# Choosing between narrow and wide matmuls while a recurrence runs: an instruction budget in the planner, and an input projection in 512 columns

## The chip, the cores and the metric

The kernel runs on one core of a Trainium2 chip. The metric is the device time of a whole execution in microseconds. A core has five engines with queues of their own: PE (TensorE, matmuls; PEld in the profile is its weight load), DVE (VectorE), ACT (ScalarE), POOL (GpSimd) and SP, which only issues DMAs here.

## The reference

The model is a two-layer transformer-like network on 16 sequences of 569 tokens with 256 channels. An image tokenizer with attention makes 441 tokens, 128 text tokens follow. Layer 0 is windowed attention and a mixture of eight experts with two picked for each token. Layer 1 is what matters here:

```python
h = h + L0_ffn(layernorm(h))            # experts: gelu(x @ W1 + b1) @ W2 + b2, two per token
# layer 1, first half: phasor memory
key   = tanh(gelu(x @ Wk1 + bk1) @ Wk2 + bk2) * freq * pi      # query alike
memory    = cumsum(exp(1j * key)[..., None] * (x @ Wv + bv)[:, :, None, :], axis=1)
retrieved = real(sum(memory * conj(exp(1j * query))[..., None], axis=2)) / sqrt(pos * K)
h = h + layernorm(retrieved) @ Wo + bo
# layer 1, second half: LSTM over 569 steps
gates = x_t @ W_ih.T + b + h_prev @ W_hh.T
i, f, g, o = split(gates, 4)
c = sigmoid(f) * c + sigmoid(i) * tanh(g)
h_t = sigmoid(o) * tanh(c)
# then, over time: prefix and suffix sums of the h_t picked by an argmax, added to 2 * h_t
```

The LSTM's step depends on the step before it, 569 times. Everything else in layer 1 works on blocks of tokens: block j of the LSTM can begin when the phasor memory has been worked out for its tokens and their input projection x @ W_ih.T lies in HBM.

## The kernel before

The kernel first does tokenizer, windowed attention and routing (until about 1000 us in the profile), then the 79 tiles of the experts (until about 1578 us), and then layer 1, in which the LSTM and the phasor memory run at the same time. The change bears on this last part.

**Work in streams.** Each piece of work is a Python generator. Before each group of instructions it yields the engine that the group needs and an assumed duration. The class `Order` is the planner: its method `run` holds a time at which each engine comes free, looks at the heads of all streams, picks the one that can start first, and lets its generator issue the instructions. The order that results is the order of the program; on the chip the engines run it with semaphores. So the planner's costs decide which instruction stands where, and nothing is decided while the kernel runs. The streams of layer 1 are `steps` (the LSTM; a chain, whose steps come first whenever they are due), two of `fronts` (gathers of the experts' results on POOL, layer norm, key and query products ek, eq, v, z), two of `backs` (scores sc, retrieval r, state update ds, output projection po, input projection xm), and `all_sums` (the sums over finished LSTM runs, fin).

**The recurrence.** The 569 tokens are split into blocks of 32, eight times 64, and 25 steps. A step (`steps`, with STEP's engines and durations) has the matmuls "hidden" (L1678: 16 in the program, each of which the chip runs as two, so 32 in the profile), "input" of the next step (L1642: identity times the projected input, 4 in the program, 8 in the profile), the two activations at L1694 and L1697, and the chain over DVE and ACT at L1700, L1706, L1713, L1716, L1719 and L1721. L1721 writes X, the hidden state that the next step's L1678 reads. The gates of a step lie in four groups of 32 PSUM partitions, so the matmuls at L1678 and L1642 are narrow: at most 32 columns of the array each.

**Narrow and wide.** A matmul whose stationary operand has 128 columns fills the array; call it wide ("128\*128" in the profile). One with 32 columns or fewer uses a quarter and can run beside three others: narrow ("128\*32", "128\*16"). The helper `product` (L1054 is its matmul) splits every product of the layer into four narrow matmuls for 32 output rows each, always. One product of 256 columns is then 8 matmuls in the profile, with 8 weight loads. Transposes (L1288, L1448, L1781) stay wide, and their yields say so ("all"). For a change of width the planner adds `FROM_TILES` and `TO_TILES` to the assumed duration of a stream's matmul, and it prefers by `SAME_TILES` what keeps the width. `self.usual`, "32" in this stage, is the width that a yield without one has.

**Fit beside the chain.** `limits` works out by when each engine is due for the chain again. A stream's instruction is taken only if it ends by then, plus `spare` (0.1 to 0.45 us for PE, set in `steps` by how far the blocks are along). The chain's own steps carry no cost for a change of width.

**Input projection.** `back` ends with the products xm: for each 128 tokens and each half of the 1024 gate columns one PSUM bank of 512 columns, filled in two parts of 256 columns, each with two products over k. DVE adds the bias (L1549, xp), and SP's queue stores the result to XPD in HBM, from where `load` in `steps` fetches the LSTM's input (xp) for eight steps.

**Gathers.** `front` fetches the experts' rows with indirect DMAs that POOL issues (L1309, yg), four for each group.

Of the kernel before, what the change touches and what calls it, by code (L numbers as in the profile page):

```python
# [109 lines left out]
COLUMN = 0.00169  # L110
# [8 lines left out]
FROM_TILES = {None: 0.0, "all": 0.0, "32": 0.18, "64": 0.19}  # L119
SAME_TILES = 0.3  # L120

AHEAD = 1.0


# [18 lines left out]
class Stream:  # L143
    def __init__(self, steps, chain=False):
        self.steps, self.chain = steps, chain
        self.head, self.ready, self.over, self.rank = None, 0.0, False, 0


class Order:
    def __init__(self, usual=None):  # L150

        self.usual = usual
        self.free = dict.fromkeys(("PE", "DVE", "ACT", "POOL", "+"), 0.0)
        self.events, self.ends = {}, dict.fromkeys(STEP, 0.0)
        self.now, self.table, self.tiles, self.chosen = 0.0, None, None, None

        self.spare = 0.1
        self.forks, self.held, self.freed = [], set(), {}
# [10 lines left out]
    def unlock(self, name):  # L169
        self.held.discard(name)  # L170
        self.freed[name] = self.now

    def past(self, event):
        return self.events.get(event, self.now + 1) <= self.now
# [47 lines left out]
    def run(self, streams, until=None):  # L222
        streams = [s if isinstance(s, Stream) else Stream(s) for s in streams]
        for s in streams:
            if s.head is None and not s.over:
                self.advance(s)
        while self.forks or not all(s.over for s in (until or streams)):
            for s in self.forks:
                self.advance(s)
            streams = [s for s in streams if not s.over] + self.forks  # L230
            self.forks = []
            for s in streams:
                self.settle(s)
            if all(s.over for s in (until or streams)):
                continue
            chain = [s for s in streams if s.chain and not self.blocked(s)]
            limit, best = {}, None
            if chain:
                limit = self.limits(chain[0])
                engine, us = STEP[chain[0].head][:2]  # L240
                start = limit[uses(engine)[0]]
                best = (start, -100, -1, chain[0], engine, us, start)
            for n, s in enumerate(streams):
                if s.chain or self.blocked(s):
                    continue
                either = s.head[0] == "DVE/ACT"
                kind = s.head[2] if len(s.head) > 2 and not either else None
                if s.head[0] == "PE":
                    kind = kind or self.usual
                for engine, us in zip(("DVE", "ACT"), s.head[1:]) if either else [s.head[:2]]:  # L250
                    other = kind != self.tiles if engine == "PE" else kind not in (None, self.table)
                    if other:
                        us += 1.3 if engine != "PE" else FROM_TILES[self.tiles] + TO_TILES[kind]
                    start = max([s.ready] + [self.free[e] for e in uses(engine)])
                    key = start + (SAME_TILES if other and engine == "PE" else 0.0)
                    end = min(limit.get(e, 1e9) for e in uses(engine))
                    spare = self.spare if engine == "PE" else self.spare / 4
                    taken = us - OVERLAP[engine.strip("+")]
                    if start + taken > end + spare and not (start > s.ready + 8.0 and start < end - 0.5):
                        continue  # L260
                    if best is None or (key, s.rank, n) < best[:3]:
                        best = (key, s.rank, n, s, engine, us, start)
            assert best is not None, "all streams wait"
            _, _, _, s, engine, us, start = best
            if s.chain:
                for e in uses(engine):
                    self.free[e] = start + us
                self.ends[s.head] = start + STEP[s.head][2]
                s.ready = start + us
                if engine == "PE":  # L270
                    self.tiles = "32"
            else:
                for e in uses(engine):
                    self.free[e] = start + (us if e == "+" else us - OVERLAP[e])
                if engine == "PE":
                    self.tiles = s.head[2] if len(s.head) > 2 else self.usual
                elif len(s.head) > 2 and s.head[0] != "DVE/ACT":
                    self.table = s.head[2]
                s.ready = start + us
            was = self.chosen = engine  # L280
            self.advance(s)
            if not s.chain and not s.over and s.head[0].strip("+") != was.strip("+"):
                s.ready += HOP + DRAIN * (was == "PE")
# [3 lines left out]
def kernel(ctx: ExitStack, tc: tile.TileContext, a: dict, out: bass.AP):  # L287
# [674 lines left out]
    Wih = l1w.tile([128, 2, 4 * D], F32, name="W_ih")  # L962
# [86 lines left out]
    def product(out, lhsT, rhs, start, stop):  # L1049


        for m in range(0, out.shape[0], 32):
            own = slice(m, min(m + 32, out.shape[0]))
            nc.tensor.matmul(out[own], lhsT[:, own], rhs, start=start, stop=stop)  # L1054

    def bank(name, slot):
        return ps.tile([128, 512], F32, name=name, tag=f"bank{slot}", bufs=1)

    plan = Order(usual="32")


    def experts(g, mo, slots):
# [367 lines left out]
    def back(p, c, batch, at, slot, late=False):  # L1430
# [5 lines left out]
        key = [PHI[:, 0, (at + j) * 128 : (at + j + 1) * 128] for j in range(2)]  # L1436
        query = [PHI[:, 1, (at + j) * 128 : (at + j + 1) * 128] for j in range(2)]

        n = 1 if c8 else 2
        block, r0, m = (len(BLOCKS) - 1, 0, 25) if late else (0, 32, 32) if c8 else (1 + c, 0, 64)  # L1440
# [14 lines left out]
        if not late:  # L1455
# [7 lines left out]
            for s in range(0 if c8 else 2):  # L1463
                half, other = (slice(64 * i, 64 * i + 64) for i in (s, 1 - s))
# [71 lines left out]
        for i in range(2 * n):  # L1536
            j, half = i // 2, i % 2
            mm = bank(f"xm{u}_{i}", slot)
            for part in range(2):
                for k in range(2):  # L1540
                    yield "PE", 256 * COLUMN
                    at_ = 512 * half + 256 * part
                    product(
                        mm[:, 256 * part : 256 * part + 256], xT[:, k, j * 128 : (j + 1) * 128],
                        Wih[:, k, at_ : at_ + 256], start=(k == 0), stop=(k == 1),
                    )
            xp = wk.tile([128, 512], F32, name=f"xp{u}_{i}", tag=f"xp{slot}", bufs=2)
            yield "DVE", 0.69
            nc.vector.tensor_tensor(xp, mm, lstm_b[:, 512 * half : 512 * half + 512], ALU.add)  # L1549

            each = 32 if c8 else 64
            for b in range(128 // each):
                nc.sync.dma_start(
                    XPD[block][:, half, 2 * (p + j) + b, :], xp[each * b : each * b + m, :]
                )
# [431 lines left out]
```

## Time and profile before

| what | us |
|---|---|
| plain runs, median of 3 (lowest, highest) | 3397.39 (3396.58, 3398.89) |
| profiled execution, whole | 3522.78 |
| profiled execution, span of the core | 3521.0 |
| PE busy, of the span | 3096.4 (48456 matmuls) |
| DVE busy / ACT busy / POOL busy | 1948.5 / 1232.6 / 756.9 |
| mean granted PE clock | 0.968 |

The profile is of one execution that is longer than the plain runs; rows of it are compared with its own span. The page lists busy time of the engines, the costliest groups (line, engine, operation, tiles and shapes, count, busy time, mean of one, idle time before and what ended it) and the chain of work that ended last. Ends of matmuls are modelled and matmuls overlap, so the mean of one (276 ns for L1678) is no rate: rates come from the distance of starts. In a line, `g<-W_hh,X 128*16 128x128 f32` is a matmul that writes g, with a stationary operand of 16 columns and a moving one of 128. A DMA queue named "instruction" carries the engines' programs: q8 moved 382 packets, 6.26 MB.

### The profile page before, as it was taken

The page shows a single profiled execution, that of the slowest core. Times are in us where ns is not written, and L with a number is a line of the kernel's source. Part 1 is how long each engine was busy: PE and PEld are TensorE (multiplying, and loading weights), DVE is VectorE, ACT ScalarE, POOL GpSimd, SP SyncE. Part 2 cuts the span into 40 slices and gives each one's busy share as a digit, 9 for nine tenths or more (in the row PEclk, how much of TensorE's full clock was granted, in tenths as well). Part 3 has the DMA queues.
Part 4 walks back from the last instruction along what each step waited for, and adds up shares of the span by engine and source line. Part 5 has one row for each costly group of instructions (what it writes and reads, how often), then busy time and mean ns, then how long its engine had stood idle before and what let it go on. Part 6 is the DMA issues. An engine that isn't in the chain of part 4 may idle for free.

```text
span 3521.0 us, 114116 instructions
## 1 busy us (share of the span) xinstructions
PE 3096.4 (88%) x48456; PEld 2277.0 (65%) x48456; DVE 1948.5 (55%) x6425; ACT 1232.6 (35%) x3944; POOL 756.9 (21%) x1343
## 2 busy tenths in 40 slices
PE   6999999899589999986888999989999999998763
PEld 3666666666478888873555667666666666666542
DVE  4677767776622111114565666666666666676445
ACT  3554455444312222213332333333333333422221
POOL 1254355533700000004322111121111111001000
PEclk8999999999799999998999999999999999999997
DMA  4111122100376666643222222322222232232303
GB/s 171 50 65 54 65 82 80 41 28 25 128 268 225 228 225 226 230 156 101 71 71 82 81 78 77 87 71 78 81 82 73 69 86 82 76 96 73 134 31 111
DMA packets 177726, 364.60 MB, mean 104 GB/s; under 512 B 25296, under 2 KB 102656, under 8 KB 164160
## 3 DMA queue, kind: packets, MB, share of 16 engines
q1 hardware_dynamic: 156240, 310.11, 27.6%
q0 software_dynamic: 13824, 37.77, 3.2%
q10 hardware_dynamic: 7152, 9.41, 0.8%
q8 instruction: 382, 6.26, 0.8%
q14 instruction: 128, 1.05, 0.1%
HBM read 238.87 MB, written 118.33 MB: 101 GB/s over the span
## 4 chain that ended last, share of the span: by engine, by line
PE 38%; DVE 8%; ACT 5%; issue 2%; another core or an unknown queue 1%; DMA 0%; POOL 0%; SPq 0%; DVEq 0%; ACTq 0%; POOLq 0%
PE g L1678 16%; PE xm_False L1054 6%; PE g L1642 2%; PE ek L1054 2%; PE z L1054 2%; ACT act L1694 2%; PE eq L1054 2%; PE po_False L1054 2%; PE r_False L1054 2%; PE v L1054 1%; DVE ab L1700 1%; ACT th L1719 1%; DVE cT L1713 1%; DVE act L1706 1%; DVE X L1721 1%
## 5 line engine op out<-in xcount | busy, mean ns | idle before, releaser
L1678 PE MATMUL g<-W_hh,X 128*16 128x128 f32 (+1 forms) x18176 | 630.8, 276 | 157.2 <-DVE X L1721 128.0
L1678 PEld LDWEIGHTS g<-W_hh,X 128*16 128x16 f32 (+1 forms) x18176 | 484.0, 104 | 324.2 <-DVE X L1721 279.0
L1694 ACT ACTIVATE act<-g 128x96 f32<-128x96 f32 x568 | 142.0, 250 | 692.8 <-PE g L1678 638.6
L1700 DVE SCALAR_TENSOR_TENSOR ab<-act 128x64 f32<-128x64 f32 x568 | 128.4, 226 | 430.2 <-ACT act L1694 413.4
L1200 ACT ACTIVATE hT<-hp,w 128x256 f32<-128x256 f32 x316 | 132.3, 471 | 476.0 <-PE hp L1193 313.0
L1207 PE MATMUL y<-w,hT 128*128 128x256 f32 x1264 | 289.8, 382 | 6.1 <-ACT hT L1200 2.5
L1054 PE MATMUL xm_False<-W_ih,dxT_False 128*32 128x256 f32 x4352 | 281.5, 381 | 9.6 <-issue 4.2
L1193 PE MATMUL hp<-xt,w 128*128 128x256 f32 x1264 | 285.7, 379 | 0.0
L1309 POOL DMA_INDIRECT yg<-YS,yat x144 | 143.5, 997 | 649.9 <-DMA YS<-ys 611.9
L1207 PEld LDWEIGHTS y<-w,hT 128*128 128x128 f32 x1264 | 236.7, 190 | 46.3 <-ACT hT L1200 15.6
L1193 PEld LDWEIGHTS hp<-xt,w 128*128 128x128 f32 x1264 | 238.9, 190 | 33.9 <-ACT hT L1200 0.2
L1719 ACT ACTIVATE th<-cT 128x32 f32<-128x32 f32 x569 | 130.6, 230 | 365.7 <-DVE toT L1716 356.6
L1642 PE MATMUL g<-xp,ident 128*32 128x128 f32 x4552 | 239.0, 276 | 14.4 <-DMA xp<-XPD 10.2
L1213 DVE TENSOR_TENSOR ys<-y,w 128x512 f32<-128x512 f32 x79 | 54.6, 692 | 351.7 <-PE y L1207 345.9
L1054 PEld LDWEIGHTS xm_False<-W_ih,dxT_False 128*32 128x32 f32 x4352 | 146.2, 110 | 85.7 <-issue 12.5
L1252 POOL TENSOR_SCALAR r_False_rstd<-r_False_mv,cols 128x2 f32<-128x2 f32 x36 | 13.4, 371 | 770.9 <-DVE r_False_mv L1247 765.7
L1721 DVE SCALAR_TENSOR_TENSOR X<-toT,th 128x32 f32<-128x32 f32 x569 | 109.5, 192 | 115.0 <-ACT th L1719 112.2
L1642 PEld LDWEIGHTS g<-xp,ident 128*32 128x32 f32 x4552 | 144.6, 111 | 33.0 <-DMA xp<-XPD 10.9
L680 PE MATMUL wqk<-wxT,wqkv 128*128 128x128 f32 x1152 | 150.5, 279 | 7.6 <-ACT wxT L674 6.6
L888 POOL DMA_INDIRECT XS<-XN,at x144 | 149.6, 1039 | 34.0 <-issue 26.6
L680 PEld LDWEIGHTS wqk<-wxT,wqkv 128*128 128x128 f32 x1152 | 141.1, 193 | 22.8 <-issue 10.4
L1549 DVE TENSOR_TENSOR xp_False<-xm_False,lstm_b 128x512 f32<-128x512 f32 x136 | 93.5, 687 | 77.7 <-PE xm_False L1054 42.9
(343 smaller groups left out, 5879.1 us busy)
## 6 DMA issues: line engine op xcount, KB each, us to landing
w<-in_wpack SPq DMA_DIRECT2D x79, 1154.0 KB
xp<-XPD SPq DMA_DIRECT2D x71, 512.0 KB
XPD<-xp_False SPq DMA_DIRECT2D x256, 128.0 KB
taps<-in_taps SPq DMA_DIRECT2D x16, 1764.0 KB
xs<-XS SPq DMA_DIRECT2D x79, 256.0 KB
YS<-ys SPq DMA_DIRECT2D x79, 256.0 KB
HD<-h SPq DMA_DIRECT2D x72, 128.0 KB
fh<-HD SPq DMA_DIRECT2D x72, 128.0 KB
```

The costliest lines, as they stand in the source:

```text
L680: nc.tensor.matmul(qk[:, j, m, :], wqkv[:, k, D * j + 128 * m : D * j + 128 * m + 128], xT[:, k, :], start=(k == 0), stop=(k == 1),)
L888: fill(0, nc.gpsimd.indirect_dma_start(out=XS[0], out_offset=bass.IndirectOffsetOnAxis(ap=at[:, i, c - lo : c - lo + 1], axis=0), in_=XN[p ...
L1054: nc.tensor.matmul(out[own], lhsT[:, own], rhs, start=start, stop=stop)
L1193: nc.tensor.matmul(hp[:, i, :], w1[:, k, hc * 128 : (hc + 1) * 128], xT[:, k, :], start=(k == 0), stop=(k == 1),)
L1207: nc.tensor.matmul(y[:, i, :], hT[:, hc, 128 * i : 128 * i + 128], w2[:, hc, :], start=(hc == 0), stop=(hc == 3),)
L1309: nc.gpsimd.indirect_dma_start(out=y, out_offset=None, in_=YS[g], in_offset=bass.IndirectOffsetOnAxis(ap=yat[:, p + j, i, c : c + 1], axis=0),
L1642: nc.tensor.matmul(g[32 * q : 32 * q + 32, :128], ident[:, 32 * (t % 4) : 32 * (t % 4) + 32], xp[:, t // 4, 128 * q : 128 * q + 128], star ...
L1678: nc.tensor.matmul(g[32 * q : 32 * q + NB * (1 + half), :128], before[:, kk, NB * (1 - half) :], Whh[:, kk, 512 * half + 128 * q : 512 * h ...
L1694: nc.scalar.activation(act[:, :96], g[:, :96], AF.Tanh, scale=0.5)
L1700: nc.vector.scalar_tensor_tensor(ab, act[:, :64].rearrange("p (g x) -> p g x", g=2), 1.0, act[:, 64:].rearrange("p (g x) -> p g x", g=2), ...
L1719: nc.scalar.activation(th.rearrange("p k x -> p (k x)"), cT, AF.Tanh, scale=0.5)
L1721: nc.vector.scalar_tensor_tensor(X[:, :, t, NB:], toT, 1.0, th, ALU.add, ALU.mult)
```

## The change

The planner gets a budget of PE's instructions, `room`: at most 120, refilled by 20 for each planned microsecond, and charged by `issue` for everything that PE is given (32 for "hidden", 8 for "input", 8 for a narrow product, 2 for a wide one or a transpose). When a stream's yield for PE names no width, it is narrow if the matmul before it was narrow and the budget holds more than half, and wide otherwise. `product` reads the width that the planner settled on. An output of fewer than 128 rows (r against the state, 64 rows) is still split in 32s. After the recurrence's own matmuls the width is "32". In `back` the input projection no longer works in parts of 256 columns: each product is 512 columns, with one yield.

```diff
+PACE, ROOM = 20.0, 120.0
 class Order:
-    def __init__(self, usual=None):
-        self.usual = usual
+    def __init__(self, narrow=False):
+        self.narrow, self.room, self.at = narrow, ROOM, 0.0
...
+    def issue(self, start, n):
+        self.room = min(ROOM, self.room + PACE * max(0.0, start - self.at)) - n
+        self.at = max(self.at, start)
...
-                if s.head[0] == "PE":
-                    kind = kind or self.usual
+                if s.head[0] == "PE" and self.narrow and kind is None:
+                    more = PACE * max(0.0, max(s.ready, self.free["PE"]) - self.at)
+                    go_on = self.tiles == "32" and min(ROOM, self.room + more) > ROOM / 2
+                    kind = "32" if go_on else "all"
...
                 if engine == "PE":
                     self.tiles = "32"
+                    self.issue(start, 32 if s.head == "hidden" else 8)
...
                 if engine == "PE":
-                    self.tiles = s.head[2] if len(s.head) > 2 else self.usual
+                    self.tiles = width
+                    self.issue(start, 8 if width == "32" else 2)
...
     def product(out, lhsT, rhs, start, stop):
-        for m in range(0, out.shape[0], 32):
-            own = slice(m, min(m + 32, out.shape[0]))
+        width = 32 if plan.tiles == "32" or out.shape[0] < 128 else 128
+        for m in range(0, out.shape[0], width):
+            own = slice(m, min(m + width, out.shape[0]))
             nc.tensor.matmul(out[own], lhsT[:, own], rhs, start=start, stop=stop)
...
-    plan = Order(usual="32")
+    plan = Order(narrow=True)
...
-            for part in range(2):
-                for k in range(2):
-                    yield "PE", 256 * COLUMN
-                    at_ = 512 * half + 256 * part
-                    product(
-                        mm[:, 256 * part : 256 * part + 256], xT[:, k, j * 128 : (j + 1) * 128],
-                        Wih[:, k, at_ : at_ + 256], start=(k == 0), stop=(k == 1),
-                    )
+            for k in range(2):
+                yield "PE", 512 * COLUMN
+                product(
+                    mm, xT[:, k, j * 128 : (j + 1) * 128], Wih[:, k, 512 * half : 512 * half + 512],
+                    start=(k == 0), stop=(k == 1),
+                )
```

More of the change, by code (lines that the diff above doesn't have):

```diff
@@ L241, in run @@
                 start = limit[uses(engine)[0]]
-                best = (start, -100, -1, chain[0], engine, us, start)
+                best = (start, -100, -1, chain[0], engine, us, start, "32")
             for n, s in enumerate(streams):
@@ L261, in run @@
                     if best is None or (key, s.rank, n) < best[:3]:
-                        best = (key, s.rank, n, s, engine, us, start)
+                        best = (key, s.rank, n, s, engine, us, start, kind)
             assert best is not None, "all streams wait"
-            _, _, _, s, engine, us, start = best
+            _, _, _, s, engine, us, start, width = best
             if s.chain:
```

## The prediction

> **What bounds the kernel now.** I read the page first, for the span and the costly groups; then the stretches of the last part of the span, for how many recurrent steps each holds and how dense TensorE's work is; then the order of time inside single steps.
>
> ```profile
> span 3521.0 us, 114116 instructions
> PE 38%; DVE 8%; ACT 5%; issue 2%; another core or an unknown queue 1%; DMA 0%; POOL 0%; SPq 0%; DVEq 0%; ACTq 0%; POOLq 0%
> L1678 PE MATMUL g<-W_hh,X 128*16 128x128 f32 (+1 forms) x18176 | 630.8, 276 | 157.2 <-DVE X L1721 128.0
> L1054 PE MATMUL xm_False<-W_ih,dxT_False 128*32 128x256 f32 x4352 | 281.5, 381 | 9.6 <-issue 4.2
> ```
>
> The 568 steps of the recurrence that end in L1721 fill 1721 to 3481 us, half of the span. A step is a closed loop: 32 matmuls at L1678, then ACT and DVE up to X at L1721, then the next 32. What the layer's other work (L1054 above all) puts on PE in between either fits into the loop's shadow or makes the step longer.
>
> How a full step and a change of width look, in order of time on PE (start, length, what):
>
> ```profile
> 2616.09 1.06 PE L1678 MATMUL g<-W_hh,X 128*16 128x128 f32 x32
> 2616.97 0.40 PE L1642 MATMUL g<-xp,ident 128*32 128x128 f32 x8
> 2617.18 0.61 PE L1054 MATMUL ds_False<-V,kT 128*32 128x256 f32 x8
> 2617.61 1.48 PE L1054 MATMUL xm_False<-W_ih,dxT_False 128*32 128x256 f32 x24
> 2618.91 1.06 PE L1678 MATMUL g<-W_hh,X 128*16 128x128 f32 x32
> ...
> 2620.43 0.61 PE L1054 MATMUL ds_False<-V,kT 128*32 128x256 f32 x8
> 2620.98 0.66 PE L1288 MATMUL dtr_False<-ident,dxn_False 128*128 128x128 f32 x4
> 2621.47 0.27 PE L1288 MATMUL ftr<-ident,fxn 128*128 128x128 f32 x1
> 2621.67 1.07 PE L1678 MATMUL g<-W_hh,X 128*16 128x128 f32 x32
> ```
>
> Starts count, since ends are modelled. 32 hidden matmuls take 0.88 us, 8 of the input 0.21, a product of 256 columns (8 narrow matmuls) 0.43; with four products the step is 2.82 us and PE is the bound. Steps with less on PE are 2.71 to 2.72 apart (2610.55 to 2613.26, say): there the loop bounds. From a narrow product to a transpose 0.55 passes instead of 0.43 (+0.12; 0.114 in nearly all cases), from a transpose to a narrow matmul 0.20 instead of 0.109 (+0.09). A pair of changes costs 0.21.
>
> Then what is lost. In this stretch table each line is a stretch, its length, and busy time and count on PE, PEld, DVE, ACT, POOL; then PE clock, DMA share, GB/s:
>
> ```profile
> 1893.00:3000.00 1107.00, 1012.31 (x23772) 728.22 (x23764) 710.73 (x2787) 411.80 (x1533) 190.72 (x344) 0.98 0.27 77
> 3000.00:3250.00 250.00, 234.15 (x5806) 169.37 (x5802) 169.71 (x663) 79.87 (x335) 22.38 (x54) 1.00 0.30 84
> ```
>
> The same stretches for the steps alone (DVE at L1721):
>
> ```profile
> 1893.00:3000.00 1107.00, 69.52 (x362) 0.98 0.27 77
> 3000.00:3250.00 250.00, 17.34 (x90) 1.00 0.30 84
> ```
>
> 362 steps at 3.058 us against 90 at 2.778. Yet the second stretch is the denser one: 23.2 narrow matmuls a microsecond against 21.5. So the count of instructions as such doesn't slow PE. What the second stretch lacks are POOL's gathers (L1309): 92 of them between 1900 and 3000, none after. One such moment, POOL and PE in order of time:
>
> ```profile
> 2337.79 0.95 POOL L1309 DMA_INDIRECT yg<-YS,yat  x1 [0.30 <-issue]
> 2339.04 0.95 POOL L1309 DMA_INDIRECT yg<-YS,yat  x1 [0.30 <-issue]
> ...
> 2337.98 0.41 PE L1678 MATMUL g<-W_hh,X 128*16 128x128 f32 x4
> 2338.71 0.41 PE L1678 MATMUL g<-W_hh,X 128*16 128x128 f32 x5 [0.33 <-issue]
> 2339.46 0.43 PE L1678 MATMUL g<-W_hh,X 128*32 128x128 f32 x5 [0.33 <-issue]
> 2340.90 0.41 PE L1678 MATMUL g<-W_hh,X 128*32 128x128 f32 x4 [1.01 <-issue]
> ```
>
> PE gets four or five matmuls out and then waits for nothing that the profile names, until the gathers end; that step took 8.8 us. The loss is 362 x (3.058 - 2.778) = 101 us, and 31 steps in the 101 us from 1722 add 101 - 31 x 2.778 = 15: 116 us. The profiled execution lasted 3522.8 us and the plain runs 3397.4, 125 less. That the two numbers nearly agree is the crux: I take it that most of this trickle belongs to the profiled execution, where each instruction also leaves a record, and that plain runs hardly have it.
>
> [...]
>
> **The change part by part.** Counts are from the built order of both kernels, durations from the trace.
>
> Width. A product of 256 columns is 8 narrow matmuls or 2 wide ones. Wide ones in the expert stage follow each other at 0.216 us (18 at L1193 from 1200.81 to 1204.69), so 2 take 0.432, as the 8 narrow ones do. Width alone is worth nothing in array time. From step 32 to step 480 the matmuls per step go from 67.0 to 56.8, with as many weight loads.
>
> Changes of width. Transitions in the layer go from 312 to 507: at the start (before the first step) 36 to 2, in steps 1 to 30 14 to 30, in the wait before step 32 14 to 10, later 248 to 466. Inside the steps that is 234 x 0.104 = 24 us more for PE. Most of it is hidden by the loop of 2.717 us. I summed each step as 0.87 for the hidden matmuls + its other matmuls + 0.104 a transition, and took 2.717 where that is less. Steps 1 to 30: 83.4 to 84.1. From 32 on: 1478.6 to 1482.1 (204 steps over 2.717 instead of 210, but 13 reach 2.85 or more where 3 did, since the planner puts less work into a step that changes). Together +4.3 us. Were the cover gone it would be the 24.
>
> Input part. Two products of 512 columns replace four of 256: the same array time (2 x 0.865), half the instructions in either width, a coarser grain to place. Both k passes now go to the whole bank; DVE's addition at L1549 waits for the last of them as before. Nothing. DMAs, POOL, SP and the gathers keep their number, and gathers are still issued by the same streams; no wait is added. The r products against the state stay narrow (64 rows), so where the planner believes in wide they are transitions; they are in the 507.
>
> Start. The recurrence stands from 1823 to 1893 for the input of its second block. PE's work before the first step, in steps 1 to 30 and in this wait goes from 82.2 + 52.5 + 50.1 to 80.9 + 49.5 + 60.1, +5.7, less 22 transitions (2.3): +3.4. PE has 50 of 70 us of work there and the rest is latency, so between 0 and 10; I take +2. Later blocks: their last input product stands 4 to 18 steps ahead of use, before 6 to 18; at step 351 one wait of 2 us at most is in the order. I leave it in the range.
>
> Fetch or trickle: 0 in plain runs (my choice), -35 in the profiled one: 49 steps of over 3 us between 1900 and 3000 make 234 us, and 15% fewer instructions at the same trickle is 35. Bounds 0 and -116.
>
> Sum: +4.3 + 2 = +6 on 3397.4: 3403. On the profiled execution 3521 + 6 - 35 = 3492.
>
> **Rivals.** (1) The trickle is in plain runs too, and gets shorter with fewer instructions: 3397 + 6 - 35 = 3368, down to 3300 were it to vanish. For it: the 101 us are plain to see and sit on PE. Against: the 125 us between profiled and plain would need another home. (2) Slower: the drains aren't hidden. It is one mechanism, the wide product that stands right before a hidden product (224 steps instead of 112 end in wide work), at the place where the planner books nothing for the recurrence's own switch. If each extra transition lands on the loop it is 24 us, and with the start's 3: 3424. It decides once some 65 of the 234 are uncovered (6.8 us). For it: fast steps between 1900 and 3000 average 2.783, above my 2.760 from sums, so work isn't always in time. (3) The budget hardly bites and nothing moves: 3397; against it, 48% of products are wide in the built order.
>
> **How the numbers follow.** Forecast 0.55 (own range 3397 to 3411), rival 1 0.22, rival 2 0.18, rival 3 0.05. Some 0.2%, 6.8 us, is what a measurement here tells from no change, and the forecast lies just inside. Faster: 0.20 of rival 1 and 0.02 of the forecast. Slower: 0.16 of rival 2 and 0.22 of the forecast. Same: the rest. The range reaches from rival 1's own figure to rival 2's.
>
> **What would show it.** Right: the profiled span falls by 20 to 40 us while the plain time doesn't; full steps after 3000 stay at 2.72 to 2.82 with some at 2.9 to 3.1; a transition still costs 0.09 to 0.12. Wrong: a plain time under 3385 (the trickle was real), or steps without gathers averaging over 2.82 (drains on the loop).

## The result, and the profile after

| | kernel before | changed kernel |
|---|---|---|
| plain runs, median of 5 (lowest, highest), us | 3397.35 (3394.94, 3398.89) | 3415.2 (3413.4, 3418.01) |
| ratio, 95% interval | | 1.0055 (1.0043 to 1.0066) |
| profiled execution, span of the core, us | 3521.0 (first), 3396.0 (a second one, below) | 3414.6 |
| PE matmuls in the profile | 48456 | 42060 |

The change costs 17.9 us. The forecast of 3403 named the side and missed two thirds of the size. The profiled span that it gave, 3492, is 77 us too long.

The page of the changed kernel, its lines for the span, for the engines on the chain that ended last, and for the two matmul groups shown of before (L1688 is the old L1678, L1066 the old L1054, L1731 the old L1721):

```profile
span 3414.6 us, 101284 instructions
PE 38%; DVE 8%; ACT 4%; issue 1%; POOL 1%; DMA 1%; SPq 0%; DVEq 0%; ACTq 0%; POOLq 0%
L1688 PE MATMUL g<-W_hh,X 128*16 128x128 f32 (+1 forms) x18176 | 606.9, 274 | 127.9 <-DVE X L1731 121.9
L1066 PE MATMUL xm_False<-W_ih,dxT_False 128*32 128x512 f32 (+1 forms) x1762 | 270.3, 594 | 1.2 <-DVE dxT_False L1237 0.5
```

There are 11% fewer instructions, the chain has the same make-up, and the input part's products at L1066 now have 512 columns in 1762 matmuls where 4352 stood. So the edit does what it says, and brings no gain.

The stretches that the prediction used, first everything, then the steps alone (DVE at L1731); columns as there:

```profile
1893.00:3000.00 1107.00, 1063.89 (x21727) 738.71 (x21723) 778.51 (x3026) 427.84 (x1627) 194.35 (x354) 1.00 0.29 83
3000.00:3250.00 250.00, 206.01 (x4833) 140.41 (x4833) 147.62 (x608) 62.12 (x299) 15.86 (x36) 1.00 0.30 98
```

```profile
1893.00:3000.00 1107.00, 75.53 (x393) 1.00 0.29 83
3000.00:3250.00 250.00, 17.07 (x89) 1.00 0.30 98
```

A step takes 1107 / 393 = 2.817 us in the first stretch, where POOL gathers (the last gather starts at 2882.0), and 250 / 89 = 2.809 in the second, where it doesn't. The 3.058 of the first profile of before is gone from the stretch with gathers. Whether the change took it away or the first profile was odd is what the first experiment asks.

Two steps of the changed kernel and the start of a third, PE in order of time (start, length, what):

```profile
2842.97 1.06 PE L1688 MATMUL g<-W_hh,X 128*16 128x128 f32 x32
2843.84 0.40 PE L1652 MATMUL g<-xp,ident 128*32 128x128 f32 x8
2844.18 1.56 PE L1066 MATMUL eq<-fxT,Wq 128*128 128x256 f32 x6
2845.57 0.38 PE L1066 MATMUL sc_False<-PHI 128*128 128x128 f32 x2
2845.89 1.07 PE L1688 MATMUL g<-W_hh,X 128*16 128x128 f32 x32
...
2848.60 1.07 PE L1688 MATMUL g<-W_hh,X 128*16 128x128 f32 x32
```

The first step has its products wide (128\*128): from one hidden product to the next 2845.89 - 2842.97 = 2.92 us. The next one, all narrow, takes 2.71. By the prediction's prices the wide step is 0.87 + 0.22 + 3 x 0.43 + 0.22 + 2 x 0.104 = 2.81. It lasts 0.11 longer than that. This 0.11 turns out to be a term that the prediction lacked.

### The profile page after: what moved, and what is told of

It reads as the page before. It is cut to its first block, busy times and chain, and to the rows that moved or that the text cites. A ratio compares the mean times of both kernels' runs of the same rounds, so it can differ in the third digit from the quotient of the medians.

```text
span 3414.6 us, 101284 instructions
## 1 busy us (share of the span) xinstructions
PE 3063.0 (90%) x42060; PEld 2234.9 (65%) x42060; DVE 1958.1 (57%) x6445; ACT 1227.2 (36%) x3928; POOL 764.0 (22%) x1343
## 4 chain that ended last, share of the span: by engine, by line
PE 38%; DVE 8%; ACT 4%; issue 1%; POOL 1%; DMA 1%; SPq 0%; DVEq 0%; ACTq 0%; POOLq 0%
PE g L1688 15%; PE xm_False L1066 6%; PE g L1652 2%; PE v L1066 2%; PE ek L1066 2%; PE z L1066 2%; PE eq L1066 2%; PE r_False L1066 2%; ACT act L1704 1%; DVE ab L1710 1%; ACT th L1729 1%; PE po_False L1066 1%; DVE cT L1723 1%; DVE act L1716 1%; PE ds_False L1066 1%
## 5 line engine op out<-in xcount | busy, mean ns | idle before, releaser
L1688 PE MATMUL g<-W_hh,X 128*16 128x128 f32 (+1 forms) x18176 | 606.9, 274 | 127.9 <-DVE X L1731 121.9
L1688 PEld LDWEIGHTS g<-W_hh,X 128*16 128x16 f32 (+1 forms) x18176 | 470.1, 103 | 322.8 <-DVE X L1731 315.2
L1066 PE MATMUL xm_False<-W_ih,dxT_False 128*32 128x512 f32 (+1 forms) x1762 | 270.3, 594 | 1.2 <-DVE dxT_False L1237 0.5
L1652 PE MATMUL g<-xp,ident 128*32 128x128 f32 x4552 | 229.7, 274 | 8.6 <-DMA xp<-XPD 8.6
L1731 DVE SCALAR_TENSOR_TENSOR X<-toT,th 128x32 f32<-128x32 f32 x569 | 109.3, 192 | 120.0 <-ACT th L1729 118.1
L1723 DVE STREAM_TRANSPOSE cT<-act 128x32 f32<-128x32 f32 x569 | 120.4, 212 | 19.3
L1197 DVE COPY xt<-xtr 128x512 f32<-128x512 f32 x79 | 51.0, 686 | 138.4 <-PE xtr L1192 138.4
```

Of the source, the lines that this page charges most:

```text
L1652: nc.tensor.matmul(g[32 * q : 32 * q + 32, :128], ident[:, 32 * (t % 4) : 32 * (t % 4) + 32], xp[:, t // 4, 128 * q : 128 * q + 128], star ...
L1688: nc.tensor.matmul(g[32 * q : 32 * q + NB * (1 + half), :128], before[:, kk, NB * (1 - half) :], Whh[:, kk, 512 * half + 128 * q : 512 * h ...
L1723: nc.vector.transpose(cT, act[:, 96:])
```

## The experiments

Three theories were on the table. Theory 1: changes of width cost more on the loop than the prediction's sum had. (A transition is such a change, from narrow to wide or back. "Drain" in the recorded texts is a name for the delay at one: in the first profile of before 0.114 us from a narrow product to a transpose, 0.094 from a transpose to a narrow matmul, and 0.104 is the mean of the two. What PE does in that time no trace shows.) Theory 2: the input part's coarse products of 512 columns are placed late and stop the recurrence at the ends of its blocks. Theory 3: neither as such; any edit that moves the planner's decisions gives another order, and the order of before is a good one among many. Theories A and B are about the first profile alone.

Step k below runs from the k-th X, counted from 0, to the next; a stop that an expectation puts "before step 95" is step 95 here, the last one ahead of a new block. "Steps 32 on" is the time from the end of the wait before step 32 (1863.05 us in the second profile of before, 1868.77 after) to the last X at L1721 or L1731 (3356.28, 3373.33). All parts of a span come from each kernel's own profiled execution. Repeated runs of one kernel spread over some 10 us. How much of that falls on a part can be seen where two kernels do the same work there: up to the experts' end, eleven kernels with one order of instructions took 1565.7 to 1574.1 us, while steps 32 on took 1493.2 in before and 1491.9 in a kernel that differs only ahead of the first step. So differences before the experts' end, and of 1 or 2 us elsewhere, aren't read.

### The kernel before, profiled again

No edit. Theory A: the long first profile is a matter of that one execution. Theory B: every profiled execution of this kernel has it.

> The kernel before, unchanged, profiled once more beside the others. Theory A (the trickle of PE's instructions during the gathers belongs to that one profiled execution): time 3397, profiled span 3390 to 3400, 1893 to 3000 us with steps of 2.78 us as after the gathers. Theory B (every profile of this kernel has it): time 3397, profiled span near 3520.

Measured: median 3397.91 (lowest 3392.03, highest 3401.4), ratio 1.0002 (0.9993 to 1.001), the profiled execution 3397.76 with a span of 3396.0. Stretches of this second profile, all engines and then the steps alone (DVE at L1721); the last gather starts at 2869.2, inside the first stretch:

```profile
1880.00:2990.00 1110.00, 1054.70 (x26076) 768.94 (x26076) 778.50 (x3054) 447.12 (x1677) 198.93 (x364) 1.00 0.30 85
2990.00:3240.00 250.00, 204.31 (x5240) 149.34 (x5236) 145.36 (x603) 62.80 (x301) 15.62 (x36) 1.00 0.30 97
```

```profile
1880.00:2990.00 1110.00, 76.36 (x398) 1.00 0.30 85
2990.00:3240.00 250.00, 17.31 (x90) 1.00 0.30 97
```

A step takes 2.789 us in the stretch with the gathers and 2.778 in the one without. One gather moment, POOL and then PE:

```profile
2326.45 1.35 POOL L1309 DMA_INDIRECT yg<-YS,yat  x1 [0.17 <-issue]
2328.10 0.95 POOL L1309 DMA_INDIRECT yg<-YS,yat  x1 [0.31 <-issue]
...
2325.63 1.07 PE L1678 MATMUL g<-W_hh,X 128*16 128x128 f32 x32 [1.43 <-DVE X L1721]
2328.38 1.07 PE L1678 MATMUL g<-W_hh,X 128*16 128x128 f32 x32 [1.47 <-DVE X L1721]
```

The 32 hidden matmuls follow each other unbroken, and the wait named is X. In the first profile they came in fours and fives with a pause after each. So theory A: the trickle belonged to one execution. Theory B falls, and with it the reason that the prediction gave, that each instruction leaves a record: this profile holds as many instructions as the first, 114116, and its queue named "instruction" moved the same 382 packets. The profiled executions of all the kernels below, and of the changed one, lie at most 8.4 us above the median of their runs too. From here on the second profile stands for before.

### One half of the change alone: the input part in 512 columns

```diff
-            for part in range(2):
-                for k in range(2):
-                    yield "PE", 256 * COLUMN
...
+            for k in range(2):
+                yield "PE", 512 * COLUMN
```

> The kernel before with the input part's products of 512 columns alone, every product narrow. Theory 1 (the change's loss of 18 us is drains at changes of width: transitions 324 here, 312 before): 3397 to 3401. Theory 2 (the coarser grain lets background work come later, so that the recurrence waits at block ends; in the built order it stands still before steps 95, 287 and 415 with 4, 12 and 7 us of other PE work): 3405 to 3415.

Measured: 3420.12, ratio 1.0066 (1.0052 to 1.0079). This half alone costs 22 us, more than both halves together, and no product changes its width. The recurrence stops at three block ends: steps 95 (5.2 us), 287 (20.0) and 415 (8.2). Steps 32 on take 29.6 us more than before, and the wait before step 32 takes 9.7 less. The worst one, with X, then the last input products on PE, their addition on DVE, the store and the load on SP's queue, and PE's input product:

```profile
2573.32 0.19 DVE L1719 SCALAR_TENSOR_TENSOR X<-toT,th 128x32 f32<-128x32 f32 x1 [0.27 <-ACT th L1717]
...
2577.25 1.92 PE L1054 MATMUL xm_False<-W_ih,dxT_False 128*32 128x512 f32 x16
2579.61 0.68 DVE L1547 TENSOR_TENSOR xp_False<-xm_False,lstm_b 128x512 f32<-128x512 f32 x1
2581.98 1.18 SPq L1551 DMA_DIRECT2D XPD<-xp_False  x2
2585.04 0.89 SPq L1628 DMA_DIRECT2D xp<-XPD  x2
2589.59 0.65 PE L1640 MATMUL g<-xp,ident 128*32 128x128 f32 x8 [3.94 <-DMA xp<-XPD]
```

X is ready at 2573.5, but the block's last input products begin only at 2577.25; addition, store and load follow, and PE stands the last 3.94 us for the DMA. The next X comes 20.0 us after the one shown. Theory 2 has the right mechanism here; the 3420 lies above its 3405 to 3415.

### The other half alone: the budget with parts of 256 columns

```diff
-            for k in range(2):
-                yield "PE", 512 * COLUMN
...
+            for part in range(2):
+                for k in range(2):
+                    yield "PE", 256 * COLUMN
```

against the changed kernel.

> The changed kernel with the input part's products of 256 columns as before, so the budget alone. Transitions in the order 684, against 508 with the whole change and 312 before. Theory 1 (drains): 684 - 312 = 372 transitions of 0.104 us are 39 us on PE, of which more shows than of the whole change's 196: 3418 or more. Theory 2 (grain): under 3410, its two stops before steps 95 and 159 alone (4 and 7 us of PE work).

Measured: 3427.85, ratio 1.0089 (1.0073 to 1.0104): 30 us for this half. Transitions go to 684, and steps 95 (5.2 us) and 159 (8.0) are stops. As theory 1 expected; theory 2, which had under 3410 here, falls as the account of the whole. But 22 and 30 don't add to 18: halves of a planner's edit can't be summed.

### The order of the changed kernel, every product narrow

```diff
-        width = 32 if plan.tiles == "32" or out.shape[0] < 128 else 128
+        width = 32
```

The planner decides as in the changed kernel, and so the order is the same; only the matmuls are narrow.

> The changed kernel in its own planned order, but every product issued as narrow matmuls again; transposes stay wide. Transitions 420 in place of 508. Theory 1 (drains): 88 x 0.104 = 9 us come back, 3404 to 3408. Theory 3 (the loss lies in the order that the planner chose, not in the widths): 3413 to 3416, as the whole change. If narrow instructions as such cost PE time in plain runs: slower than 3415.

Measured: 3416.07, ratio 1.0053 (1.0039 to 1.0067). The changed kernel itself is at 1.0055. So all the widths together, gains and costs, are worth nothing that can be told, and the order alone brings the loss, as theory 3 has it. Theory 1, which expected 3404 to 3408 here, falls as the account of the net loss. Inside, the widths do move time. They save 3.8 us before the first step (138.4 instead of 142.2), and from step 32 on the changed kernel takes 6.0 more (1504.6 against 1498.6). Not all of the 6.0 is shown to be width: in three stretches of 3.4 us in the changed kernel's trace (from 2064.4, 2149.7 and 2699.2) the granted PE clock was 0.5, and the steps in them (102, 132, 327) took 3.56 to 3.57 us, where those of the narrow order, at full clock, took 2.77, 2.74 and 3.06. That is 2.1 of the 6.0; whether the widths bring these stretches is open. The same steps that were shown of the changed kernel, narrow:

```profile
2842.75 1.06 PE L1688 MATMUL g<-W_hh,X 128*16 128x128 f32 x32
2843.63 0.40 PE L1652 MATMUL g<-xp,ident 128*32 128x128 f32 x8
2843.84 1.48 PE L1066 MATMUL eq<-fxT,Wq 128*32 128x256 f32 x24
2845.14 0.40 PE L1066 MATMUL sc_False<-PHI 128*32 128x128 f32 x8
2845.46 1.07 PE L1688 MATMUL g<-W_hh,X 128*16 128x128 f32 x32
```

2.71 us instead of 2.92. The sum of this step's matmuls is 2.60, and the loop of 2.717 bounds it. A wide block that cost 2 x 0.104 would make it 2.81; it made it 2.92, so it cost 0.31 or 0.32.

### The widths in the order of before

The planner of before, which takes every product as narrow, decides the order; a budget beside it decides only the physical width.

```diff
+                    more = PACE * max(0.0, start - self.at)
+                    go_on = self.width == "32" and min(ROOM, self.room + more) > ROOM / 2
+                    self.width = s.head[2] if len(s.head) > 2 else "32" if go_on else "all"
+                    self.issue(start, 8 if self.width == "32" else 2)
...
+        width = 32 if plan.width == "32" or out.shape[0] < 128 else 128
```

> The order of the kernel before, instruction group by instruction group, with 256 columns in the input part; only whether a product is issued as narrow or wide matmuls follows the budget. 690 transitions in the order instead of 312, no stop of the recurrence at a block's end. Theory 1 (drains on the loop): the sum over steps from 32 on goes from 1478.6 to 1509.8, the start gets 4 us shorter, so about 3398 + 31 - 4 = 3425. Theory 3 (only the order matters): 3394 to 3402.

Measured: 3448.3, ratio 1.0148 (1.0132 to 1.0164). Transitions go from 312 to 690, steps 32 on from 1493.2 to 1541.7 us, the rest of the span by some 4. Theory 3's number is missed by some 50 us and theory 1's by 23: with the order held, widths that the planner doesn't pay for cost 48.5 us for the 392 extra transitions that the traces have from step 32 on (640 instead of 248), 0.12 each, more than the prediction's 0.104, although some are hidden. Two neighbouring steps with the same work show why. The first is wide, the second narrow:

```profile
2672.89 1.07 PE L1691 MATMUL g<-W_hh,X 128*16 128x128 f32 x32
2673.77 0.40 PE L1655 MATMUL g<-xp,ident 128*32 128x128 f32 x8
2674.11 1.99 PE L1067 MATMUL xm_False<-W_ih,dxT_False 128*128 128x256 f32 x8
2676.03 1.07 PE L1691 MATMUL g<-W_hh,X 128*16 128x128 f32 x32
2676.91 0.40 PE L1655 MATMUL g<-xp,ident 128*32 128x128 f32 x8
2677.13 1.91 PE L1067 MATMUL xm_False<-W_ih,dxT_False 128*32 128x256 f32 x32
2678.86 1.06 PE L1691 MATMUL g<-W_hh,X 128*16 128x128 f32 x32
```

3.14 against 2.83: four products of 256 columns in either, and 0.31 more where they are wide. The trace's single starts say where it goes. The wide block begins 0.114 later than a narrow one would after the input product. The hidden product begins 0.309 after the last wide start instead of 0.216, 0.093 more. And between these, the second wide product starts 0.320 after the first, where all later ones start after 0.216: 0.104 more. Together 0.311. This extra belongs to the wide blocks that begin with two products of 256 or 512 columns after a narrow matmul: the 10th and the 90th percentile of that distance are both 320 ns in the changed kernel (103 cases), here (221), and with every product wide (234); with 512 columns 533 or 534 instead of 429 to 432. For two transposes it is mostly 0.164 instead of 0.109 (108 cases in the first profile of before, 84 in the changed kernel).

The kernel before has no wide product among the steps, only transposes. The view that the prediction took its price from (narrow to transpose, transpose to narrow) couldn't show the 0.104. It did show the transposes' own share: the four at 2620.98 take 0.49 us to the next start where 4 x 0.109 is 0.44, so that a pair of changes around transposes costs 0.26, not 0.21.

To see how far this carries, the prediction's sum by steps was made again from the traces: 0.87 + the other matmuls + 0.104 a transition, at least 2.717, and then also 0.104 for the second product of each wide block (0.055 for a second transpose). Steps 32 on, without the one or two steps of over 4 us, in us:

| kernel | measured | sum, prediction's prices | left over | sum with the second product | left over |
|---|---|---|---|---|---|
| before, second profile | 1488.9 | 1475.8 | 13.1 | 1476.9 | 12.0 |
| changed kernel | 1499.3 | 1476.8 | 22.5 | 1486.0 | 13.3 |
| its order, narrow | 1493.4 | 1475.5 | 17.9 | 1478.1 | 15.3 |
| budget, parts of 256 | 1507.6 | 1477.9 | 29.7 | 1494.6 | 13.0 |
| widths in the order of before | 1532.9 | 1504.3 | 28.6 | 1522.5 | 10.4 |
| every product wide (below) | 1532.1 | 1497.5 | 34.6 | 1523.2 | 8.9 |

With the prediction's prices the remainder runs from 13 to 35 us and grows with the wide blocks; with the one extra term it stays between 9 and 15 for all six. That is a mis-sized price found and priced. It is no full account of an order: summed in the same way (within some 2 us), the other traces leave 12 us (wide only before the first step) to between 16 and 24 (the rest), the most with the planner's constants changed, where no product is wide.

### Wide only before the first recurrent step

```diff
-        for m in range(0, out.shape[0], 32):
...
+        width = 32 if plan.ends["hidden"] or out.shape[0] < 128 else 128
```

in the kernel before.

> The kernel before, with wide products until the first step of the recurrence and narrow ones from then on: order unchanged, transitions 278 instead of 312, all 34 of them before the first step. If drains before the first step lie on its chain, 34 x 0.104 = 3.5 us less: 3394. If they are hidden in latencies there: 3398.

Measured: 3395.17, ratio 0.9997 (0.9989 to 1.0006): not told from before. The time to the first X stays (135.4 us instead of 135.8). In this order the widths ahead of the first step are hidden, and the 3.8 us that they save in the changed kernel's order only take back part of what that order loses.

### Two constants of the planner, no change of width

```diff
-COLUMN = 0.00169
+COLUMN = 0.00172
```

> The kernel before with one constant of the planner changed, the assumed time of a column from 0.00169 to 0.00172 us; the work is the same and every product narrow. Theory 3 (the loss comes from where the greedy planner happens to leave the background behind the recurrence): in this order the recurrence stops before steps 95, 159, 287 and 415 with 4, 11, 7 and 6 us of other PE work, the sum from step 32 on goes from 1478.6 to 1494.7: 3410 to 3418, as large as the change's loss, with no change of width in it. If order at this scale doesn't matter: 3398.

```diff
-SAME_TILES = 0.3
+SAME_TILES = 0.2
```

> The kernel before with another constant of the planner changed, the preference for the same width from 0.3 to 0.2 us: 332 transitions instead of 312, no stop at a block's end in the order, sum from step 32 on 1479.1 instead of 1478.6. Theory 3: 3397 to 3401, since no stop appears. If any other order than that of before costs 10 to 20 us: 3408 or more.

Measured: 3449.38, ratio 1.0156 (1.0142 to 1.017), and 3416.2, ratio 1.0056 (1.0042 to 1.007). With the larger COLUMN the recurrence stops at four block ends (steps 95, 159, 287, 415: 5.1, 15.1, 11.1 and 9.8 us); more than theory 3 expected, but 18.6 us of the loss lie before it, since the experts end at 1590.6 us instead of 1572.0: the constant moved the earlier part too (PE's order differs from 139 us on). With the smaller SAME_TILES the order differs from 77 us on, the experts end 10.5 us later, and steps 32 on take 7.5 more, with no stop. Theory 3 as put here, by stops alone, had 3397 to 3401; what came is its wider form, that nearly any other order costs 10 to 20 us. A planner's constant changed by 2% costs three times what the change under study costs.

### More slack for the planner, before

```diff
-            plan.spare = 0.0 if ahead else 0.2 if done >= 4.0 * u / BLOCKS[j][1] - AHEAD else 0.45
+            plan.spare = 0.0 if ahead else 0.25 if done >= 4.0 * u / BLOCKS[j][1] - AHEAD else 0.45
```

> The kernel before with the planner's middle allowance for PE at 0.25 instead of 0.2 us, which acts in the part with the recurrence alone: every product narrow, 324 transitions instead of 312, one stop (before step 95, 4 us), sum from step 32 on 1483.5 instead of 1478.6. If the sums over the built order tell the time: 3402 to 3405. Theory 3: 3408 or more.

Measured: 3411.61, ratio 1.0044 (1.0031 to 1.0058), where the sums by step said 3402 to 3405. One stop (step 95, 5.2 us), and steps 32 on at 1509.9, 16.7 more than before. As theory 3 has it, before's order is better than this neighbour. The trace shows a part of it that no sum over PE's work can hold. In steps 273, 337 and 401 another stream's load of an activation table on ACT stands ahead of the recurrence's activation th. In step 273:

```profile
2543.09 1.28 ACT L1343 ACT_TABLE_LOAD   x1
2543.49 0.21 DVE L1713 STREAM_TRANSPOSE cT<-act 128x32 f32<-128x32 f32 x1
2544.38 0.47 ACT L1343 ACTIVATE gk<-ek,cols 128x256 f32<-128x256 f32 x1
2544.75 0.22 ACT L1719 ACTIVATE th<-cT 128x32 f32<-128x32 f32 x1
2545.00 0.19 DVE L1721 SCALAR_TENSOR_TENSOR X<-toT,th 128x32 f32<-128x32 f32 x1 [0.29 <-ACT th L1719]
```

Its operand cT is done at 2543.70, and th begins at 2544.75. The three steps take 3.65 or 3.66 us where 2.72 is usual; five such steps are in the kernel with the larger COLUMN, none in before, in the changed kernel or in its narrow order.

### The budget set loose, and set to nothing

In the changed kernel, first so much room that recurrent steps rarely fall to wide; then the same with the background held a little earlier; then no narrow choice at all:

```diff
-PACE, ROOM = 20.0, 120.0
+PACE, ROOM = 80.0, 400.0
```

> The changed kernel with a budget that never runs out (400, refilled by 80 a microsecond): products stay narrow after the recurrence's matmuls and become wide only after a transpose, until the recurrence's next matmuls. 236 transitions in place of 508, 62.4 matmuls a step in place of 56.8, one stop at a block's end (before step 95, 6 us of other PE work), sum from step 32 on 1481.3 in place of 1482.1. Theory 1 (drains at the end of a step's work are what the change pays): the steps that end in wide work fall back to about 100, and 8 us come back: 3403 to 3409. Theory 3 (any order other than that of before costs 10 to 20 us, whatever its transitions): 3412 to 3420.

```diff
-AHEAD = 1.0
+AHEAD = 0.9
```

> The same kernel with a budget that never runs out, and the planner's AHEAD at 0.9 instead of 1.0, which removes the stop: 248 transitions, sum from step 32 on 1481.8, 46 us of PE work in the wait for the second block instead of 54. Theory 1: 3395 to 3402, level with the kernel before. Theory 3: 3408 or more.

```diff
-                    kind = "32" if go_on else "all"
+                    kind = "all"
```

> The changed kernel with every unnamed width wide (the budget never allows narrow), so nearly every step ends in wide work: 1082 transitions, 48.0 matmuls a step, one stop (before step 223, 3 us), sum from step 32 on 1501.6. Theory 1: the sum gives +23 us against before and some 330 more steps that end in wide work give 0.08 each, 26: 3437 to 3450. If fewer instructions helped in plain runs, it would be the fastest of all, under 3398.

Measured, by rising number of transitions: 3405.59 with 236, ratio 1.0027 (1.0017 to 1.0037); the changed kernel's 3415.2 with 508; 3452.74 with 1082, ratio 1.0158 (1.0144 to 1.0172). With AHEAD at 0.9 it is 3399.64, ratio 1.0003 (0.9994 to 1.0011), level with before; its profiled execution was its longest, so its parts aren't compared. Theory 1 expected the two loose budgets about where they came, and theory 3 missed both (3412 to 3420, and 3408 or more): not every other order costs 10 us. Loose limits leave few wide products beside the recurrence (66 wide matmuls of products from step 32 on against 830 in the changed kernel; in all, 4 wide blocks begin with two products of the same columns against 139), and the time is 9.6 us below the changed kernel's. Since the order differs too, this alone doesn't say how much of that is width. With every product wide it is somewhat above what theory 1 expected. The kernel with the fewest matmuls (37608) is, with that of the larger COLUMN, the slowest of all, so fewer PE instructions as such bought nothing here. One of its steps, with two products of 512 columns:

```profile
2501.77 1.07 PE L1688 MATMUL g<-W_hh,X 128*16 128x128 f32 x32
2502.65 0.40 PE L1652 MATMUL g<-xp,ident 128*32 128x128 f32 x8
2502.98 1.98 PE L1066 MATMUL xm_False<-W_ih,dxT_False 128*128 128x512 f32 x4
2504.90 1.07 PE L1688 MATMUL g<-W_hh,X 128*16 128x128 f32 x32
```

3.13 us, with 4 wide matmuls. The same work narrow is 16 matmuls and 0.87 + 0.22 + 2 x 0.865 = 2.82 (0.865 is an estimate, twice the 0.43 of 256 columns; in the changed kernel narrow products of 512 columns start 0.858 or 0.859 apart): the wide block's 0.31 again.

No kernel here beats before beyond doubt. The nearest are wide only before the first step (0.9997) and the loose budget with AHEAD at 0.9 (1.0003).

## Why the prediction came out as it did

**Where the 17.9 us went.** Spans differ by 3414.6 - 3396.0 = 18.6:

| part of the span, us | before | changed | its order, narrow |
|---|---|---|---|
| until the experts end | 1572.0 | 1573.7 | 1572.0 |
| to the first X | 135.8 | 138.4 | 142.2 |
| steps 0 to 30 | 89.5 | 90.0 | 91.1 |
| wait before step 32 | 65.8 | 66.6 | 67.1 |
| steps 32 on | 1493.2 | 1504.6 | 1498.6 |
| after the last X | 39.7 | 41.3 | 40.8 |

From the first column to the third the order alone adds 15.7 us, 9.3 of it between the experts' end and step 32, and 5.4 from there to the last X. From the third to the second 5.4 come back before step 32 and 6.0 are added after, of which 2.1 fall into the stretches at half clock. The rest lies outside these parts or within their spread. So the loss is an order's loss, into which the widths' gain and cost have been folded. Why this order takes 6.4 us longer to the first X was not followed up.

**The bound and the trickle.** That plain runs hardly have the trickle was right: of 17.9 us nothing points to it, and a kernel of 3397 us has a profile of 3396.0 without it. The reason given was an estimate, from 116 us of loss beside 125 us between the profiled and the plain time, and it was wrong. It wasn't profiling as such, it was that one execution. Hence the -35 us for the profiled span failed: 3414.6 instead of 3492, and a fall of 106 from 3521.0, of which the change has no part. Rival 1 falls.

**Width.** "Width alone is worth nothing in array time" holds for the pitch (0.216 for a wide matmul of 256 columns; in the traces of before and of the changed kernel four narrow ones start 6 to 7 ns apart, side by side, and the next four 0.216 after them), and not for a block, whose second product is 0.104 late.

**From step 32 on: the term that was too small.** The prediction took a pair of changes at 0.208 from transposes and got +3.5 us from step 32 on (1478.6 to 1482.1); 11.4 was measured. A wide block of products costs 0.311. With that the sums over the traces say +9.1 in place of +1.0 for the steps under 4 us, and 10.4 was measured. The method of summing each step against 2.717 left 9 to 15 us over in the six kernels of the table; for them its price was too small. (The four counts of transitions that the prediction lists add up to 508, not 507.)

The narrow order splits the 11.4 in another way: 5.4 are there without a wide product, for which the prediction's prices give nothing (1475.8 to 1475.5), and 6.0 come with the widths. So two things failed: the price of a wide block, and the reading of the sums as the time of an order. The second is the larger one in the whole span.

**Input part: "Nothing".** As an edit to array time, yes. As an edit to what the planner places it is +22 us alone and -13 beside the budget (3427.85 to 3415.2). The prediction read the built order of the changed kernel, which had no stop like that of 20 us, so for the sum little was missed; as a statement on this part it is wrong.

**Start and waits.** +2 was forecast (0 to 10); to the first X, in steps 0 to 30 and in the wait it is 2.6 + 0.5 + 0.8 = 3.9. That it came so near is in part luck: the prediction had +5.7 for PE's work and -2.3 for transitions, and the runs show +9.3 for the order and -5.4 with the widths. Steps 1 to 30 also stand in its sum twice, here and among the steps. The stop at step 351 came, 5.3 us for a step of 2.7, so 2.6 where 2 at most was said; before has a step 32 of 4.3 us that the changed kernel doesn't have, so that the net is 1.0.

**Rivals.** Rival 2 had the right side and a nearby place: uncovered changes of width on the loop. Its price, each of 234 extra transitions at 0.104, was not how it went: many are covered, and the ones that aren't cost more than 0.104. In the profile 211 of the steps from 32 on end in wide work instead of 106, and they run over their sums by 14.4 instead of 6.0 us. With the second product priced both are between 5 and 6, for twice as many steps in the changed kernel, so that nothing is left that speaks for the place as such. What the planner would do if it booked the recurrence's own switch is open: it was not tried. Rival 3 fell, as 139 wide blocks and 18 us show.

**Chances.** The forecast's own range, 3397 to 3411, was too narrow above: it took a change of order as free wherever the sums agreed. The 3415.2 lies nearer to rival 2's 3424 than to the forecast's 3403; the wide range, which reaches from one rival's figure to the other's, covers it without telling why. None of its signs told this either: a kernel slower by changes of width was to show as steps without gathers over 2.82 us on average, and they took 2.809, up from 2.778. The experiments on the planner's constants moved the same kernel by 14 to 53 us with no edit to the work.

## What to carry to other kernels

Price a change of tile width with the operation that will make it, from starts in a trace, and count the second instruction of the new width too: the two changes at transposes gave 0.21 us, a block of wide products costs 0.31. Where a planner decides the order, the halves of an edit can't be priced apart, and an edit that costs nothing in array time can still move 20 us through what is placed late; compare with the same order at the old width before blaming the width, and look at the other engines of the chain too, since a sum over PE's work doesn't see a table load on ACT (1.28 us in the step shown). Profile a kernel a second time before reading an effect from a profiled execution that is longer than its plain runs.

## What the runs showed of the hardware

After a narrow matmul the second of two wide 256-column products in fp32 starts 0.320 us after the first instead of 0.216, in the three traces counted above. In the records, the first wide weight load begins together with its matmul (2674.103 and 2674.105 us), while later ones begin a whole pitch ahead of theirs (2674.427 for 2674.641). In the changed kernel's 103 such blocks the first load leads its matmul by 0 to 2 ns and the second by 0.212 to 0.214 us. That an uncovered load is the cause is a reading of these, not shown by a run.

One execution of the kernel before, the first profiled, took 3522.78 us, with PE handing out four or five matmuls at a time beside POOL's gathers. It did not come back in the second profile, nor in any run of the kernel before beside the experiments (highest 3403.23). The granted clock at the moment that the prediction shows was 1.00 until 2341 us and 0.50 from 2342 on, after the trickle had begun, so a low clock didn't start it. What caused it stays open.
